# Steps to 1/std, the end of a convolution, and the halves of layer 3's convolutions: three edits in one kernel of four layers

## The chip, the cores and the metric

The kernel runs on one core of a Trainium2 chip. A core has five engines that run side by side, each through its own list of instructions in order: TensorE (PE in the profile; its weight loads are listed apart as PEld), VectorE (DVE), ScalarE (ACT), GpSimd (POOL) and SyncE (SP), which here only issues transfers. Transfers run on the core's 16 DMA engines. The engines meet through semaphores, and the profile shows for an idle engine what ended its wait.

The metric is the device time of one execution in microseconds, so lower is better. Three runs of the kernel before took 3970.76, 3970.90 and 3973.34 us; the median is 3970.9.

## The reference

`x` has the shape (1, 512, 64, 64) in fp32. Four layers follow one another, each a group norm, a function and a residual:

```python
def _gn(v, G=32, eps=1e-5):          # 32 groups of 16 channels, over all pixels
    m = jnp.mean(g, axis=(2, 3, 4), keepdims=True)
    s = jnp.var(g, axis=(2, 3, 4), keepdims=True)
    return ((g - m) / jnp.sqrt(s + eps)).reshape(v.shape)

x = x + L0(_gn(x)); x = x + L1(_gn(x)); x = x + L2(_gn(x)); x = x + L3(_gn(x))
```

- **L0** is attention with 8 heads of 64 over the 4096 pixels. Its scores are -(|q|^2 + |k|^2 - 2 q.k) / 8; q, k, v and the output are 1x1 convolutions of 512 to 512 channels.
- **L1 and L2** are gated convolutions. A 1x1 convolution takes 512 channels to 1024: the first 128 are `pwa`, the other 896 go through a 7x7 depthwise convolution and are cut into 128, 256 and 512 (`dw0`, `dw1`, `dw2`). Then `h = pwa * dw0`, `h = pw0(h) * dw1`, `h = pw1(h) * dw2`, and the layer's output is `w_out(h)`.
- **L3** is a linear attention. A 1x1 convolution takes 512 channels to 768, with a scale and a bias for each channel; a 5x5 depthwise convolution of these, with its own scales and biases, gives 768 more. Of the 1536, the first 512 are q, the next k, the last v; `q = relu(q) + eps`, `k = relu(k) + eps`. Then `vk` = sum over the pixels of v k^T, `attn = (vk q) / z` with `z` from the mean of k and q, `y = attn * g + bt + v`, and a 1x1 convolution `w_proj` of y with a scale and a bias.

The pointwise biases are inputs too, and there is no affine part in the group norms.

## The kernel before, in words

**What stays on chip.** `X` (128 partitions, 4 chunks of channels, 4096 pixels) holds the activations through all layers. A block is 512 pixels, of which there are eight.

**A layer's start.** `bn_stats` of every block were taken as the blocks of the layer before were finished. `_group_params` (L91) joins them (`bn_aggr`), has TensorE average them over each group of 16 channels with the constant matrix `gmask`, copies the mean out of PSUM (L100), forms the variance in three small VectorE operations (L105 to L107), sends it through `gmask` again, adds eps (L111), takes the square root on ScalarE (L113) and the reciprocal on VectorE (L115), and sharpens it in four small operations (L117 to L121). The product's input is not normalised: 1/std goes into the weights, one multiplication for each group of 128 output channels (L426 in layer 0, L819 in layers 1 and 2, L1021 in layer 3), the first on VectorE and the others on GpSimd. The mean is subtracted from `X` in place (`_Centered`, L319), block by block. `known` is called when the mean is there: it makes `less`, the negative mean (L335), centers the four chunks of the first block (two on ScalarE, two on GpSimd, L345 and L347), and adds the mean to `offset` (L338), from which the last layer gives it back. Later blocks are centered as they come up: on VectorE and ScalarE in layer 0, on ScalarE in layers 1 and 2, on VectorE in layer 3.

**Depthwise convolutions on TensorE** (`_PlaneConv`, L631). The image of a channel is cut into planes, with a border. A product over the input channels is evicted from PSUM into a `plane` tile (L843 on VectorE in layers 1 and 2; L1035 on ScalarE in layer 3) and written to DRAM from ScalarE's queue (`F` in layers 1 and 2, `G` in layer 3, L681). `load` (L686) fetches from there for two rounds of a convolution: the taps `T` (L690) and the pixels `S` (L707), both issued by SyncE. The 128 partitions of `S` are four groups of 32: two sets of channels, and for each set two shifts of the pixels. In layers 1 and 2 the second shift (in x) is a copy on ScalarE within `S` (L713); in layer 3 the second shift is in y, one tile row of taps lower, and is fetched from DRAM by a transfer of its own, so that a load there is one transfer of `T` and four of `S`. There are four buffers of each, and loads are issued one set ahead. `conv` (L721) runs the matmuls of 64 rows by 32 columns into two PSUM tiles, turns these into the right layout on VectorE (L767), and at its end goes over the result in four quarters: a transposition on VectorE (L773 in layers 1 and 2, L776 in layer 3) and a bias on ScalarE (L902, L1058). It is a generator: at each `yield` its caller puts other work between the convolution's matmuls.

**The order.** A tile scheduler orders the instructions of every engine, except the matmuls that go through `pc.matmul` (L657), which keep the order of the program. So which product stands between which parts of a convolution is written out by hand. In layers 1 and 2 `convolve` (L896) does it: there are seven convolutions, and the items of `between` (input products for the next convolutions, gates, output products) are dealt out evenly over `parts` slots, eight of them, one at each `yield`; seven lie between loads or turns and the last one behind the four quarters. After the seventh convolution the remaining gates and the output products of chunks 5 and 6 follow.

In layer 3 a convolution is one of six chunks `i` in one of two tile rows `hf`, written `(i, hf)`; it has two halves, one for each pair of PSUM tiles, each with two loads the loads of the first unit in a call of `convs` (L1065) are issued as it begins, those of each further unit while the one before it runs. `fill(n)` (L1047) makes the next n products of `w_qkv` with their planes; `made` has them chunk by chunk, in pairs for chunks 0 to 3. `gather(hf, q)` (L1081) takes a quarter of a tile row: it reads k's planes back (`row`), and gives four steps, each of which transposes k and v on TensorE (`ps_t`), evicts them (`kT` on ScalarE, `vT` on VectorE), makes a product with `w_proj` (`pv`, ScalarE, then added to `X` on GpSimd) and adds v k^T into four standing PSUM tiles (`vkp`). `added` (L1134) prepares the constant part of the output with 16 small products. The order of layer 3 is

```python
fill(20)
convs([(0, 0), (1, 0)], fills(3, 3, 3, 3))
fill(2)
convs([(2, 0), (3, 0), (4, 0)], fills(2, 2, 2, 2, 3, 3))
convs([(0, 1), (5, 0)], [added])
for q, units in enumerate(((1,), (2,), (3, 4), (5,))):
    convs([(i, 1) for i in units], gather(0, q))
```

so that all twelve convolutions have begun before the last quarter of tile row 0 is gathered, and the gathering of tile row 1 follows with no convolution beside it.

Of the kernel before, what the change touches and what calls it, by code (L numbers as in the profile page):

```python
# [16 lines left out]
P = 128  # L17
# [73 lines left out]
def _group_params(nc, small, psum, stats, gmask, known=None):  # L91


    mv = small.tile([P, NC, 2], FP, tag="gn_mv", name="gn_mv")
    for c in range(NC):
        nc.vector.bn_aggr(mv[:, c, :], stats[:, c, :, :].rearrange("p b s -> p (b s)"))
    ps = psum.tile([P, BLK], FP, tag="mm", name="gn_ps")
    nc.tensor.matmul(ps[:, 0:NC], gmask, mv[:, :, 0], start=True, stop=True)
    mean = small.tile([P, NC], FP, tag="gn_mean", name="gn_mean")
    nc.vector.tensor_copy(mean, ps[:, 0:NC])  # L100
    if known is not None:
        known(mean)

    d = small.tile([P, NC], FP, tag="gn_d", name="gn_d")
    nc.vector.tensor_sub(d, mv[:, :, 0], mean)  # L105
    nc.vector.tensor_mul(d, d, d)
    nc.vector.tensor_add(d, d, mv[:, :, 1])  # L107
    ps = psum.tile([P, BLK], FP, tag="mm", name="gn_ps")
    nc.tensor.matmul(ps[:, 0:NC], gmask, d, start=True, stop=True)
    a = small.tile([P, NC], FP, tag="gn_a", name="gn_a")  # L110
    nc.vector.tensor_scalar(a, ps[:, 0:NC], GN_EPS, None, ALU.add)  # L111
    s = small.tile([P, NC], FP, tag="gn_s", name="gn_s")
    nc.scalar.activation(s, a, AF.Sqrt)  # L113
    r = small.tile([P, NC], FP, tag="gn_r", name="gn_r")
    nc.vector.reciprocal(r, s)  # L115

    t = small.tile([P, NC], FP, tag="gn_t", name="gn_t")  # L117
    nc.vector.tensor_mul(t, r, r)
    nc.vector.tensor_mul(t, t, a)
    nc.vector.tensor_scalar(t, t, -0.5, 1.5, ALU.mult, ALU.add)  # L120
    nc.vector.tensor_mul(r, r, t)  # L121
    return mean, r


@with_exitstack
# [193 lines left out]
class _Centered:  # L319
# [10 lines left out]
    def first(self, view):  # L330


        def known(mean):
            self.less = self.small.tile([P, NC], FP, tag="less", name="less")
            self.nc.vector.tensor_scalar(self.less, mean, -1.0, None, ALU.mult)  # L335
            for c in range(NC):
                self.take(view(c), c, self.nc.gpsimd if c > 1 else self.nc.scalar)
            self.nc.vector.tensor_add(self.offset, self.offset, mean)  # L338

        return known  # L340

    def take(self, xs, c, eng):
        less = self.less[:, c : c + 1]
        if eng is self.nc.scalar:
            eng.activation(xs, xs, AF.Identity, bias=less)  # L345
        else:
            eng.tensor_scalar(xs, xs, less, None, ALU.add)  # L347


def _normalize(tc, X, gmask, small, psum, st):  # L350

    nc = tc.nc
    for b in range(NB):
        for c in range(NC):
            nc.vector.bn_stats(st[:, c, b, :], X[:, c, ts(b, BLK)])
    mean, rstd = _group_params(nc, small, psum, st, gmask)
    for b in range(NB):
        for c in range(NC):
            xs = X[:, c, ts(b, BLK)]
            nc.vector.tensor_scalar(  # L360
                xs, xs, mean[:, c : c + 1], rstd[:, c : c + 1], ALU.subtract, ALU.mult
            )


# [4 lines left out]
def _attention_pairs(tc, a, X, QO, gmask, small, centered, stats, okay):  # L369
# [19 lines left out]
    with tc.tile_pool(name="att1", bufs=1) as p1, tc.tile_pool(  # L389
# [32 lines left out]
        def project(pair):  # L422
            w = p1.tile([P, 3, NC, P], FP, tag="wqkv", name=f"wqkv{pair}")
            nc.sync.dma_start(out=w, in_=a["L0_wqkv"][pair])
            for n in range(3):
                eng = nc.vector if (pair, n) == (0, 0) else nc.gpsimd  # L426
                eng.tensor_tensor(
                    w[:, n], w[:, n], rstd.unsqueeze(2).to_broadcast([P, NC, P]), ALU.mult
                )
            Q = QO[pair]  # L430
            sq = []
            for b in range(NB):
                cols = ts(b, BLK)
                if pair == 0 and b:
                    for c in range(NC):
                        centered.take(X[:, c, cols], c, nc.scalar if c > 1 else nc.vector)
                if b % 2 == 0:
                    sq.append(ptp.tile([P, 2 * BLK], FP, tag="pt", name="sq"))
                for n in range(2):
                    ps = ps_s.tile([P, 2 * BLK], FP, tag="s", name="ps_qk")[:, 0:BLK]  # L440
                    for c in range(NC):
                        nc.tensor.matmul(  # L442
                            ps, w[:, n, c, :], X[:, c, cols], start=(c == 0), stop=(c == NC - 1)
                        )
                    if n == 0:
                        nc.scalar.activation(Q[:, cols], ps, AF.Copy, scale=2 * scale * gain_in)  # L446
                    else:
                        nc.vector.tensor_scalar(K[:, cols], ps, gain_in, None, ALU.mult)
                nc.scalar.activation(sq[-1][:, ts(b % 2, BLK)], Q[:, cols], AF.Square)
                ps = ps_s.tile([P, 2 * BLK], FP, tag="s", name="ps_v")[:, 0:BLK]  # L450
                for i in range(QT):
                    for c in range(NC):
                        nc.tensor.matmul(
                            ps[:, ts(i, P)],
                            X[:, c, ts(b * QT + i, P)],
                            w[:, 2, c, :],
                            start=(c == 0),
                            stop=(c == NC - 1),
                        )
                nc.vector.tensor_scalar(  # L460
                    V[:, ts(b, QT), :].rearrange("p t d -> p (t d)"), ps, gain_in, None, ALU.mult
                )
# [168 lines left out]
class _PlaneConv:  # L631
# [54 lines left out]
    def load(self, i, hf, wT, r):  # L686
# [4 lines left out]
            out=w.rearrange("p r g b m -> p r (g b m)"),  # L691
            in_=wT[i, r : r + nl].rearrange("r p x -> p r x"),
        )
        run = (f.part + f.by - 1) * f.fw
        S = self.sp3.tile([P, nl, 4, run], FP, tag="S", name="S")
        F = self.F[i]
        chan = f.planes * f.plane
        for rho in range(2):
            for jy in range(f.jy):
                src = bass.AP(  # L700
                    F.tensor,
                    F.offset
                    + (rho * f.nr + r) * 4 * f.ch * chan
                    + (hf * f.part + jy * f.by) * f.fw,
                    [[f.plane, 32], [f.ch * chan, 4 * nl], [1, run]],
                )
                nc.sync.dma_start(  # L707
                    out=S[ts(2 * rho + jy, 32)].rearrange("p r g n -> p (r g) n"), in_=src
                )
            if f.jx == 2:  # L710
                flat = S.rearrange("p r g n -> p (r g n)")
                n = 4 * nl * run - f.bx
                nc.scalar.copy(flat[ts(2 * rho + 1, 32), 0:n], flat[ts(2 * rho, 32), f.bx : f.bx + n])  # L713
        return w, S

    def ahead(self, i, hf, wT, r0=0):
# [4 lines left out]
    def conv(self, i, hf, wT, finish, dst, primed=False):  # L721
# [48 lines left out]
        for q in range(4):  # L770
# [7 lines left out]
                    self.turned[:, :, ts(q, f.phx), :].rearrange("p b l c -> p l b c"),  # L778
                )
            finish(d)  # L780
        yield


@with_exitstack
def _gated_convs(ctx, tc, a, X, vcol, gmask, small, new_stats, centered, stats, F):
# [12 lines left out]
    for layer in ("L1", "L2"):  # L798
# [16 lines left out]
        )  # L815
        stats = new_stats()

        def scaled(w, eng):
            eng.tensor_tensor(w, w, rstd.unsqueeze(2).to_broadcast([P, NC, P]), ALU.mult)  # L819
            return w  # L820

        scaled(w_in[0], nc.vector)
        for w in w_in[1:] + [w_gate]:
            scaled(w, nc.gpsimd)

        def product(w, hs):
            ps = ps_mm.tile([P, BLK], FP, tag="mm", name="ps")
# [8 lines left out]
        def fused(i, k):  # L836

            if i == 0 and k:
                for c in range(NC):
                    centered.take(pc.pixels(X[:, c, :], k), c, nc.scalar)  # L840
            pc.take(
                i, k, taking(w_in[i], k),
                lambda dst, src: nc.vector.tensor_scalar(  # L843
# [1 line left out]
                ),  # L845
            )
            if k == NB - 1 and len(w_in) < NDW:
                w_in.append(scaled(weights("w_in", 1 + len(w_in)), nc.gpsimd))

        D = {}  # L850

# [44 lines left out]
        def convolve(i, first, between):  # L896
# [8 lines left out]
            pc.ahead(i, 0, taps)  # L905
            for f in first:
                f()
            parts = FORM.nr // FORM.run
            done = 0
            for part, _ in enumerate(pc.conv(i, 0, taps, bias, D[i], True)):  # L910
                upto = len(between) * (part + 1) // parts
# [21 lines left out]
def _linear_attention(ctx, tc, a, X, vcol, vall, ident, gmask, small, centered, stats, F, Z, out):  # L933
# [49 lines left out]
    with ExitStack() as st:  # L983
# [33 lines left out]
                pc.matmul(ps, w(c), h, start=(c == 0), stop=(c == len(hs) - 1))  # L1017
            return ps

        def scaled(w, eng):  # L1020
            eng.tensor_tensor(w, w, rstd.unsqueeze(2).to_broadcast([P, NC, P]), ALU.mult)  # L1021

        for i, w in enumerate(w_qkv):
            scaled(w, nc.gpsimd if i else nc.vector)

        def fused(i, k):

            if i == 0 and k:
                for c in range(NC):
                    centered.take(pc.pixels(X[:, c, :], k), c, nc.vector)  # L1030
            w = w_qkv[i]
            ps = product(lambda c: w[:, c, :], [pc.pixels(X[:, c, :], k) for c in range(NC)])
            pc.take(
                i, k, ps,
                lambda dst, src: nc.scalar.activation(  # L1035
                    dst, src, AF.Identity,
                    bias=vcol(pre + "b_qkv", i), scale=vcol(pre + "s_qkv", i),
                ),
            )
            if k == NB - 1 and len(w_qkv) < NQKV:  # L1040
                w_qkv.append(weights(len(w_qkv)))
                scaled(w_qkv[-1], nc.gpsimd)

        made = [(i, k) for p in (0, 2) for k in range(NB) for i in (p, p + 1)]
        made += [(i, k) for i in (4, 5) for k in range(NB)]
# [105 lines left out]
        fill(20)  # L1151
        convs([(0, 0), (1, 0)], fills(3, 3, 3, 3))
        fill(2)
        convs([(2, 0), (3, 0), (4, 0)], fills(2, 2, 2, 2, 3, 3))
        convs([(0, 1), (5, 0)], [added])
        for q, units in enumerate(((1,), (2,), (3, 4), (5,))):
            convs([(i, 1) for i in units], gather(0, q))

        km = wp.tile([P, NC], FP, tag="km", name="km")
# [185 lines left out]
```

## Time and profile before

| | us |
|---|---|
| median of three runs | 3970.9 |
| the profiled execution | 3972.97 |
| its span (first to last instruction) | 3971.3 |
| TensorE busy | 3880.2 |
| VectorE busy | 2276.4 |
| ScalarE busy | 1871.9 |
| GpSimd busy | 95.6 |
| DMA: bytes moved | 232.84 MB |

The profiled execution had a mean granted TensorE clock of 0.989 of full speed. Its stages, by the first matmul of each layer: layer 0 begins at 36.05 us, layer 1 at 2306.33, layer 2 at 2817.53 and layer 3 at 3332.82; the last layer ends with the span.

How to read it: TensorE is busy for nearly the whole span, so the other engines' busy shares say little by themselves. What matters is where TensorE stands still or runs at less than full clock, and which instruction, on which engine, released it. The rows of stretches used below give for each engine the busy time with the number of instructions in brackets, and at the end the granted TensorE clock, the mean busy share of the DMA engines and GB/s. Rows of a timeline give the start, the duration, the engine, the line, the operation and its operands; in square brackets stands how long the engine had waited and for what.

### The profile page before, as it was taken

To read this page: it belongs to the slowest core of one execution; us is meant where nothing else is said; L and a number is where in the kernel's file an instruction comes from. 1 tells how busy PE (TensorE), PEld (TensorE's weight loads), DVE (VectorE), ACT (ScalarE), POOL (GpSimd) and SP (SyncE) were. 2 spreads that over 40 slices of the span, in tenths; PEclk is the share of its full clock that TensorE was granted. 3 is DMA by queue.
4 is the path that set the end of the run, shared out by engine and by line. 5 is a ranking of instruction groups with operands and counts; after the bars stand their busy time and mean duration, and the time that the engine had idled before them with its cause. 6 is when DMAs were issued, how large, how long until landed. Compare 5 with 4: busy or idle time off the path is not lost. (4 is left out here: it accounts for less than half of the span.)

```text
span 3971.3 us, 81238 instructions
## 1 busy us (share of the span) xinstructions
PE 3880.2 (98%) x35666; PEld 1732.5 (44%) x35666; DVE 2276.4 (57%) x2490; ACT 1871.9 (47%) x2678; POOL 95.6 (2%) x86
## 2 busy tenths in 40 slices
PE   6999999999999999999999989999999999989999
PEld 3533345333353333443333345554455544445544
DVE  4577763777727777547667623466434665233335
ACT  2577753777726777446656444441344521222210
POOL 0000000000000000000000010000000001001110
PEclk9999999999999999999999999999999999989999
DMA  2000000000000000000000045651256511696234
GB/s 96 9 2 1 1 1 9 1 1 1 1 1 9 1 2 1 1 9 1 1 1 1 1 145 163 179 144 46 85 154 179 157 45 51 178 213 142 72 92 143
DMA packets 240456, 232.84 MB, mean 59 GB/s; under 512 B 14921, under 2 KB 205641, under 8 KB 239969
## 3 DMA queue, kind: packets, MB, share of 16 engines
q1 hardware_dynamic: 213424, 168.82, 16.5%
q10 hardware_dynamic: 26640, 58.72, 4.1%
q8 instruction: 282, 4.62, 0.5%
q14 instruction: 78, 0.63, 0.1%
q0 software_dynamic: 32, 0.06, 0.0%
HBM read 167.76 MB, written 59.77 MB: 57 GB/s over the span
## 5 line engine op out<-in xcount | busy, mean ns | idle before, releaser
L495 ACT ACTIVATE pt<-ps_s,A 128x512 f32<-128x512 f32 x2048 | 1284.7, 686 | 556.4 <-PE ps_s L487 528.5
L566 DVE TENSOR_TENSOR acc<-acc,pt 128x1024 f32<-128x1024 f32 x960 | 1175.4, 1224 | 331.9 <-ACT pt L495 306.2
L505 PE MATMUL av<-pt,V 64*64 64x512 f32 x8192 | 1112.3, 590 | 0.9 <-ACT pt L495 0.9
L487 PE MATMUL ps_s<-O,K 64*64 64x512 f32 x8192 | 1111.4, 589 | 0.0
L505 PEld LDWEIGHTS av<-pt,V 64*64 64x64 f32 x8192 | 339.6, 133 | 557.4 <-issue 525.6
L487 PEld LDWEIGHTS ps_s<-O,K 64*64 64x64 f32 x8192 | 334.1, 133 | 554.1 <-issue 308.7
L713 ACT COPY S<-S 32x1295 f32<-32x1295 f32 x224 | 284.2, 1269 | 295.9 <-DMA S<-F 233.4
L657 PE MATMUL ps<-X,w_in_L 128*128 128x512 f32 x896 | 406.5, 606 | 6.8 <-DMA pw_L<-in_L_pw_dram 4.4
L657 PE MATMUL ps_cv<-S,T 64*32 64x128 f32 x13824 | 242.7, 277 | 15.4 <-DMA S<-G 14.7
L657 PEld LDWEIGHTS ps<-X,w_in_L 128*128 128x128 f32 x896 | 167.1, 192 | 206.8 <-issue 196.3
L843 DVE TENSOR_SCALAR plane<-ps,vec 128x512 f32<-128x512 f32 x112 | 83.4, 748 | 301.2 <-PE ps L657 230.4
L657 PEld LDWEIGHTS ps_cv<-S,T 64*32 64x32 f32 x13824 | 199.5, 107 | 122.9 <-issue 75.2
L442 PE MATMUL ps_qk<-X,wqkv 128*128 128x512 f32 x512 | 228.1, 599 | 5.6 <-issue 5.6
L657 PE MATMUL ps<-h,w_out_L 128*128 128x512 f32 x512 | 227.9, 598 | 0.0
L657 PE MATMUL ps<-X,w_qkv 128*128 128x512 f32 x384 | 170.7, 603 | 5.2 <-DVE w_qkv L1021 5.2
L767 DVE STREAM_TRANSPOSE turned<-ps_cv 128x512 f32<-128x512 f32 x48 | 31.6, 697 | 226.6 <-PE ps_cv L657 226.6
L345 ACT ACTIVATE X<-X,less 128x512 f32<-128x512 f32 x78 | 49.5, 708 | 230.1 <-DVE less L335 218.5
L657 PE MATMUL ps<-h,pw_L 128*128 128x512 f32 x320 | 149.3, 619 | 7.4 <-DVE X L881 6.2
L446 ACT ACTIVATE O<-ps_qk 128x512 f32<-128x512 f32 x32 | 19.1, 597 | 272.5 <-PE ps_qk L442 272.5
L442 PEld LDWEIGHTS ps_qk<-X,wqkv 128*128 128x128 f32 x512 | 95.9, 192 | 116.9 <-issue 116.9
L657 PEld LDWEIGHTS ps<-h,w_out_L 128*128 128x128 f32 x512 | 95.0, 190 | 114.6 <-issue 106.5
L865 DVE SCALAR_TENSOR_TENSOR h<-ps,vec,h 128x512 f32<-128x512 f32 x112 | 82.4, 745 | 104.7 <-PE ps L657 101.4
(129 smaller groups left out, 2540.3 us busy)
## 6 DMA issues: line engine op xcount, KB each, us to landing
T<-in_L_T_dram SPq DMA_DIRECT2D x112, 384.0 KB, 3.9
F<-plane ACTq DMA_DIRECT2D x112, 324.0 KB, 2.9
S<-F SPq DMA_DIRECT2D x224, 162.0 KB, 4.3
S<-G SPq DMA_DIRECT2D x192, 136.0 KB, 4.3
row<-G SPq DMA_DIRECT2D x80, 272.0 KB, 4.0
G<-plane ACTq DMA_DIRECT2D x48, 289.0 KB, 2.9
T<-in_L_T_dram SPq DMA_DIRECT2D x48, 256.0 KB, 4.3
out_dram<-y SPq DMA_DIRECT2D x32, 256.0 KB, 2.1
```

Source lines behind the costliest of these rows:

```text
L345: eng.activation(xs, xs, AF.Identity, bias=less)
L442: nc.tensor.matmul(ps, w[:, n, c, :], X[:, c, cols], start=(c == 0), stop=(c == NC - 1))
L446: nc.scalar.activation(Q[:, cols], ps, AF.Copy, scale=2 * scale * gain_in)
L487: nc.tensor.matmul(ps[ts(half, D), ts(h, BLK)], K[rows, t * P + half * D : t * P + (half + 1) * D], QO[pair][rows, cols], start=True, stop ...
L495: nc.scalar.activation(pt[:, ts(h, BLK)], ps[:, ts(h, BLK)], AF.Exp, bias=A[:, t, h : h + 1])
L505: nc.tensor.matmul(av[half][rows, :], V[keys, t, rows], pt[keys, ts(h, BLK)], start=(t == 0), stop=(t == NT - 1),)
L566: nc.vector.tensor_add(acc, acc, pt)
L657: self.tc.keep_in_program_order(self.nc.tensor.matmul(*args, **kw))
L713: nc.scalar.copy(flat[ts(2 * rho + 1, 32), 0:n], flat[ts(2 * rho, 32), f.bx : f.bx + n])
L767: nc.vector.transpose(out, src)
L843: lambda dst, src: nc.vector.tensor_scalar(dst, src, vcol(pre + "b_in", 1 + i), None, ALU.add),
L865: nc.vector.scalar_tensor_tensor(d, ps, bias, d, ALU.add, ALU.mult)
```

## The change

**Steps to 1/std.** `less` is read from PSUM at once, in place of the copy of the mean; the variance adds it in place of subtracting the mean. `known` is called after the second product with `gmask`. The first block's chunks are centered by ScalarE (two), GpSimd and VectorE (one each), all later blocks by ScalarE in every layer, layer 3 included. `offset` is kept up by `began`, called after the first weight is scaled. The other weights are scaled on ScalarE, in four activations of 128 columns with a scale for each partition, where before one operation on GpSimd did it (in layer 0 the later pairs of heads stay on GpSimd). Layer 3's planes are evicted on VectorE in place of ScalarE.

**Layer 3's second tile row of taps.** A load fetches each set's pixels once, 153 KB in place of two transfers of 136 KB, and ScalarE copies them, shifted by a row of taps, to the other 32 partitions. The convolutions of tile row 0 are all done in one call, and those of tile row 1 are spread over the four quarters of the gathering.

**A convolution's end.** In layers 1 and 2 there is a `yield` after each of the four quarters, and the items between are dealt out over 11 slots in place of eight.

```diff
-    mean = small.tile([P, NC], FP, tag="gn_mean", name="gn_mean")
-    nc.vector.tensor_copy(mean, ps[:, 0:NC])
-    if known is not None:
-        known(mean)
+    less = small.tile([P, NC], FP, tag="gn_less", name="gn_less")
+    nc.vector.tensor_scalar(less, ps[:, 0:NC], -1.0, None, ALU.mult)
...
-    nc.vector.tensor_sub(d, mv[:, :, 0], mean)
+    nc.vector.tensor_add(d, mv[:, :, 0], less)
...
     nc.tensor.matmul(ps[:, 0:NC], gmask, d, start=True, stop=True)
+    if known is not None:
+        known(less)
...
-            self.less = self.small.tile([P, NC], FP, tag="less", name="less")
-            self.nc.vector.tensor_scalar(self.less, mean, -1.0, None, ALU.mult)
+            self.less = less
             for c in range(NC):
-                self.take(view(c), c, self.nc.gpsimd if c > 1 else self.nc.scalar)
-            self.nc.vector.tensor_add(self.offset, self.offset, mean)
+                self.take(view(c), c, (None, None, self.nc.gpsimd, self.nc.vector)[c])
...
+    def began(self):
+        self.nc.vector.tensor_sub(self.offset, self.offset, self.less)
...
+    def scaled(self, w, rstd, eng):
+        if eng is self.nc.scalar:
+            for c in range(NC):
+                eng.activation(w[:, c], w[:, c], AF.Copy, scale=rstd[:, c : c + 1])
+        else:
+            shape = [P, NC, w.shape[-1]]
+            eng.tensor_tensor(w, w, rstd.unsqueeze(2).to_broadcast(shape), ALU.mult)
+        return w
...
-                eng = nc.vector if (pair, n) == (0, 0) else nc.gpsimd
-                eng.tensor_tensor(
-                    w[:, n], w[:, n], rstd.unsqueeze(2).to_broadcast([P, NC, P]), ALU.mult
+                centered.scaled(
+                    w[:, n], rstd, nc.gpsimd if pair else nc.scalar if n else nc.vector
                 )
+            if pair == 0:
+                centered.began()
...
-        run = (f.part + f.by - 1) * f.fw
+        run = (f.part + f.by - 1 + (f.jy - 1) * f.by) * f.fw
...
+        step = f.bx if f.jx == 2 else f.by * f.fw
+        n = 4 * nl * run - step
         for rho in range(2):
-            for jy in range(f.jy):
...
+            nc.sync.dma_start(
+                out=S[ts(2 * rho, 32)].rearrange("p r g n -> p (r g) n"), in_=src
+            )
+            nc.scalar.copy(flat[ts(2 * rho + 1, 32), 0:n], flat[ts(2 * rho, 32), step : step + n])
...
             finish(d)
-        yield
+            if f.parts == 1 or q == 3:
+                yield
...
-            scaled(w, nc.gpsimd)
+            centered.scaled(w, rstd, nc.scalar)
...
-            parts = FORM.nr // FORM.run
+            parts = FORM.nr // FORM.run + 3
...
-            scaled(w, nc.gpsimd if i else nc.vector)
+            centered.scaled(w, rstd, nc.scalar if i else nc.vector)
+        centered.began()
...
-                    centered.take(pc.pixels(X[:, c, :], k), c, nc.vector)
+                    centered.take(pc.pixels(X[:, c, :], k), c)
...
-                lambda dst, src: nc.scalar.activation(
-                    dst, src, AF.Identity,
-                    bias=vcol(pre + "b_qkv", i), scale=vcol(pre + "s_qkv", i),
+                lambda dst, src: nc.vector.tensor_scalar(
+                    dst, src, vcol(pre + "s_qkv", i), vcol(pre + "b_qkv", i), ALU.mult, ALU.add
                 ),
...
-        convs([(2, 0), (3, 0), (4, 0)], fills(2, 2, 2, 2, 3, 3))
-        convs([(0, 1), (5, 0)], [added])
-        for q, units in enumerate(((1,), (2,), (3, 4), (5,))):
+        convs([(2, 0), (3, 0), (4, 0), (5, 0)], fills(2, 2, 2, 2, 6) + [added])
+        for q, units in enumerate(((0,), (1, 2), (3,), (4, 5))):
             convs([(i, 1) for i in units], gather(0, q))
```

## The prediction

> **What bounds the kernel now.** I read the page first, then a table of stretches, then the timeline inside the bad stretches. The page's busy time:
>
> ```profile
> PE 3880.2 (98%) x35666; PEld 1732.5 (44%) x35666; DVE 2276.4 (57%) x2490; ACT 1871.9 (47%) x2678; POOL 95.6 (2%) x86
> ```
>
> TensorE sets the end, so an edit is worth only the PE idle time, or half-speed PE time, that it takes away. Idle is 3971.3 - 3880.2 = 91 us. The stretches (length, then busy us of PE, PEld, DVE, ACT, POOL, then PEclk, DMA share, GB/s) show where:
>
> ```profile
> 0.00:41.55 41.55, 6.65 (x11) 3.44 (x12) 32.38 (x70) 12.68 (x19) 9.06 (x14) 1.00 0.64 229
> 2292.81:2311.41 18.60, 6.20 (x11) 3.19 (x11) 5.99 (x20) 10.89 (x18) 9.82 (x9) 0.63 0.61 208
> 2717.78:2724.42 6.64, 4.55 (x15) 1.81 (x10) 6.59 (x7) 2.96 (x3) 0.00 (x0) 1.00 0.37 98
> 2724.42:2731.25 6.83, 5.82 (x7) 2.52 (x8) 3.50 (x6) 1.57 (x2) 0.00 (x0) 0.50 0.01 3
> 3322.77:3338.82 16.05, 6.95 (x12) 3.32 (x12) 15.66 (x43) 1.54 (x3) 10.08 (x9) 0.57 0.36 132
> 3530.61:3566.20 35.59, 24.12 (x548) 18.14 (x544) 17.80 (x30) 6.51 (x8) 0.00 (x0) 0.54 1.12 216
> ```
>
> Three kinds of place: the steps to 1/std before a layer, the end of a layer's last convolution (2717, 3232), and layer 3's convolutions at 3530, where DMA runs at a share over 1. In the last three rows PEclk near 0.5 is half speed. Timeline, VectorE, steps to 1/std of layer 3:
>
> ```profile
> 3326.90 0.89 DVE L347 TENSOR_SCALAR X<-X,less 128x512 f32<-128x512 f32 x1
> 3327.71 0.14 DVE L111 TENSOR_SCALAR gn_a<-gn_ps 128x4 f32<-128x4 f32 x1
> 3327.77 1.97 DVE L347 TENSOR_SCALAR X<-X,less 128x512 f32<-128x512 f32 x3
> 3329.67 0.16 DVE L115 RECIPROCAL gn_r<-gn_s 128x4 f32<-128x4 f32 x1
> ```
>
> The Sqrt ended at 3328.09, yet the reciprocal starts 1.6 us later, behind three centerings of X. Timeline at the end of layer 1's last convolution:
>
> ```profile
> 2720.22 4.59 DVE L773 STREAM_TRANSPOSE h<-h 128x1024 f32<-128x1024 f32 x4
> 2725.43 1.22 PE L657 MATMUL ps<-h,pw_L 128*128 128x512 f32 x1 [3.10 <-DVE X L881]
> ```
>
> Four transpositions in a row hold the evictions; PE runs out of its four PSUM buffers for 3.10 us. SyncE's queue in layer 3:
>
> ```profile
> 3545.05 0.39 SPq L690 DMA_DIRECT2D T<-in_L_T_dram  x1
> 3545.66 2.75 SPq L707 DMA_DIRECT2D S<-G  x4
> ```
>
> One load of taps and pixels per 4 us (eight from 3535 to 3567), where half a convolution, which takes two loads, computes for 2.05 us.
>
> **What the skill says.** "TensorE: Matmul & The Clock Gate" (What's actually happening): the clock halves after an idle window of 3.4 us, the windows run free. The trace agrees: half-speed stretches of 6.83, 10.24, 13.65 and 34.13 us. So a gap costs itself plus about 3 us. "GPSIMD Engine Reference" (Specifications): its SBUF interface is shared with VectorE. Agrees: the same weight scaling takes VectorE 0.69 us at 2816.69, 1.50 at 2304.72 while GpSimd scales. "DMA: Bandwidth & Descriptors" (Specifications) puts line rate at 512 B and more; here 544 B packets of S took 28 ns at 3405-3440, 49 ns at 3535-3580.
>
> **Part 1, steps to 1/std.** In the built order, VectorE keeps one centering (X, chunk 3) ahead of the square; the rest goes to ScalarE, as do the other weights' scalings, four ACTIVATEs of 128 columns each. From Sqrt to first matmul undisturbed is 2817.53 - 2815.38 = 2.15 us (layer 2).
> - Layer 0: Sqrt is bound by ScalarE: 28.25 + two centerings 1.33 + table load 1.28 = 30.9. First matmul 33.05 against 36.05: -3.0.
> - Layer 3: 25.37 add; one centering holds 0.4 to 0.8; matmul near 26.4; +0.68 and +0.17 as before: Sqrt 27.25, matmul 29.4 against 32.82: -3.4 (-3.2 to -3.6).
> - Layer 1: Sqrt 0.25 earlier (still behind the table load); scaling 0.69 for 1.50: -1.05.
> - Layer 2: saved 0.2 against the centering's 0.4: 0 (+-0.2).
> Sum -7.5. The added ACTIVATEs: "ScalarE: Activation LUTs" (What ACT_TABLE_LOAD costs) gives 186 + 93 + 0.833 N ns, 93 overlapped: an estimate of 0.29 us each, 16 of them 4.7 us; no row shows this size, the 128x512 centering is 0.708. Costed at nothing: a block of four products lasts 3.44 us on PE (6.9 at half speed), ScalarE's work for it is 4 x 0.617 + 0.33 = 2.8. The tightest is the next block's last centering: layer 1 ready 2310.5, wanted 2311.7; layer 2, behind the issue of a plane, 2826.0 against 2826.6. Uncovered it costs up to 2 us each. Evictions of q, k, v planes move from ScalarE (0.78) to VectorE (0.75), which is free then.
>
> **Part 2, convolution ends.** Yields after each quarter put output products between the transpositions; VectorE's order follows. Layer's last convolution: 15 products (0.86 us each) stand after its last rows, VectorE: turns 1.94, then 4 x 1.13 and 15 x 0.6 in groups 1,3,3,4,4. Product n waits for eviction n-4: the sum of PE waits is 0.7, none over 0.5. So 3.1 becomes 0.7, and half speed (5.8 us busy, 2.9 lost) goes: -5.3. The end of the sixth convolution, 12 products: 1.4 for 0.61; of the fourth, eight products of 0.86: 0.9 for 0. Net -3.6 per layer, -7.2 for two. What is thinned out elsewhere: between loads of layers 1 and 2 PE has 4.1 us and more on average, the load needs 2.5 us of ScalarE's copies and 3.3 of DMA (708 KB at 212 GB/s), and four buffers are full at a start: nothing.
>
> **Part 3, layer 3.** A load was four S transfers of 136 KB; now two of 153 KB and two ScalarE copies of 1207 elements, 1.19 us each (1.269 for 1295). DMA time by packets: before (1024 x 49 + 256 x 73)/16 = 4.3 us, after (512 x 51 + 256 x 73)/16 = 2.8; SyncE issues 1.4 for 2.35; ScalarE 2.4. So 4.0 us per load becomes 2.8. But convolution 5's planes are now complete only t (its last product) and its loads queue on SyncE behind three `row` transfers that wait for the same planes: planes land t+4.1, rows 4.7, taps and first S 2.8, plus 1: t+12.6; copies: first load usable t+14.2, then one per 2.4, fourth t+21.4. The second load of (0,1) is copied after convolution 5's four affines in ScalarE's order, which wait for VectorE's turns and transpositions (7 us after its end): its end t+32. Without waits it would be t+12.65: 19.3 lost. Before, 35.59 us held 4.43 + 4 x 2.05: 23.0 lost. Earlier, (2,0) to (4,0): before the halves took 0.9, 0.9, 2.5 and 1.3 too long, 5.6. After, the starts of (2,0) and (4,0) need fresh planes, then transfer, then copies: 2.1 and 4.5, the others nothing: 6.6. Net -2.6. After that, each half has a step of 7.74 us beside it and ScalarE 7.3 of 9.8 us: kT and pv stand behind copies, kT has 3.4 us of slack under the `w_proj` products: nothing; uncovered, up to 2 us per step.
>
> **Sum.** -7.5 - 7.2 - 2.6 = -17.3 against the profiled execution: span 3971.3 (time 3973.0, 1.7 around it) to 3954. That execution is 2.1 over the median of the runs, 3970.9; I take the difference from the median: 3953.6, so **3954**.
>
> **Rivals.**
> - B, the transfers really go under: saturated packets at 49 ns fall back to 28, copies keep up, 14 of the 19.3 vanish. For: 33% fewer bytes where DMA share is 1.12. Against: fresh planes and rows come first. 3940.
> - C, layer 3 turns against it: copy waits for transfer, transfer waits for buffer, both in order; 4 us per load again and longer starts, 8 us over before: -7.5 - 7.2 + 8: 3964.
> - E, the conv ends give nothing: the evictions are spread into many short waits, half speed stays: -17.3 + 7.2: 3961.
> - D, slower: in the 16 steps of the gather, ScalarE waits on a copy while kT stands behind it, PE then waits for kT. Each step would have to lose 1.6 us to pass +8 in all; at 2 us, 32 - 14.7 = +17: 3988. Against it: copies have two halves (19.6 us) of lead.
>
> **How the numbers follow.** Chances: forecast 0.52 (own range 3948 to 3960), B 0.17, C 0.13, E 0.10, D 0.08. Range 3938 to 3966 leaves out D and part of B and C. 0.2% (8 us) is about what a measurement tells from no change: faster 0.80 (forecast, B, E and little of C), same 0.12, slower 0.08.
>
> **What would show it.** First matmul near 33.0; starts of layers 1 to 3 at -1, 0, -3.4 relative to their last product; no PE gap over 1 us at the layers' last convolutions and no half-speed stretch of 6.83 there; S transfers of 153 KB, 96 of them, and 96 copies of 1.19 us; PE waiting in layer 3 on ScalarE's S instead of DMA S, some 20 us in one place after the last w_qkv product. It is wrong if PE waits in the gather on kT, or if ScalarE's scalings hold the first blocks.

## The result and the profile after

The changed kernel took 3967.47 us (median of 14 runs, 3965.76 to 3970.76), the kernel before, run beside it, 3969.83 (14 runs, 3963.32 to 3973.34). The ratio is 0.9996 with a 95% interval of 0.9988 to 1.0003: no difference that can be measured. The forecast was 3954.

The profiled execution of the changed kernel took 3965.76 us, its span is 3964.0, which is 7.3 us less than that of before. But the profile of before came from a run 3 us over its median and that of after from one 1.7 us under its own, so most of these 7.3 us are a difference between two executions. First the page's busy times of the changed kernel:

```profile
PE 3871.1 (98%) x35666; PEld 1727.7 (44%) x35666; DVE 2290.3 (58%) x2496; ACT 2001.5 (50%) x2852; POOL 65.7 (2%) x61
```

TensorE's idle time is 3964.0 - 3871.1 = 92.9 us; it was 91. What was taken away in some places has come back in others. The same table of stretches as before (length, busy us of PE, PEld, DVE, ACT, POOL, then PEclk, DMA share, GB/s), for the changed kernel:

```profile
0.00:38.15 38.15, 6.68 (x11) 3.48 (x12) 25.05 (x56) 11.47 (x22) 4.09 (x11) 1.00 0.69 249
2289.31:2304.60 15.29, 4.06 (x9) 2.41 (x9) 5.49 (x20) 7.85 (x19) 3.06 (x3) 0.67 0.54 172
2568.07:2590.00 21.93, 19.21 (x522) 11.41 (x529) 9.21 (x12) 13.08 (x11) 0.00 (x0) 1.00 0.70 191
2710.33:2723.98 13.65, 13.51 (x35) 5.39 (x31) 13.59 (x19) 4.06 (x4) 0.00 (x0) 1.00 0.10 30
3316.84:3328.60 11.76, 5.60 (x11) 2.78 (x11) 5.10 (x22) 7.93 (x20) 3.99 (x5) 0.71 0.52 180
3520.71:3551.71 31.00, 18.30 (x421) 14.26 (x417) 13.97 (x24) 21.94 (x21) 0.00 (x0) 0.59 0.67 168
```

The first, second and fifth rows are the starts of layers 0, 1 and 3, shorter than before. The fourth is the end of layer 1's last convolution: 13.51 us of 13.65 busy at full clock, where before PE stood still for 3.1 us and then ran at half speed. The third is new: in the middle of layer 1, where PE never waited before, it is idle for 2.7 us of 22. In the last row, ahead of layer 3's gathering, the DMA share has fallen to 0.67 from 1.12, and ScalarE is busy for 22 us of 31. The place (called the hole below) is 31.0 us long for 35.6, but it holds three halves of convolutions for four.

A layer's start is from the last product of the layer before to the first product of this one, its body from there to its last product, both worked out from the matmuls' times in the trace:

| stretch | before, us | after, us | measured | forecast |
|---|---|---|---|---|
| start of layer 0 | 36.05 | 32.61 | -3.4 | -3.0 |
| start of layer 1 | 13.52 | 12.35 | -1.2 | -1.05 |
| body of layer 1 | 504.64 | 504.96 | +0.3 | -3.6 |
| start of layer 2 | 6.56 | 6.70 | +0.1 | 0 |
| body of layer 2 | 505.24 | 503.52 | -1.7 | -3.6 |
| start of layer 3 | 10.04 | 6.91 | -3.1 | -3.4 |
| body of layer 3 | 638.44 | 640.28 | +1.8 | -2.6 |

The starts are right to 0.2 us in their sum (-7.6 for -7.5). The bodies failed: +0.4 for -9.8. Each column is one profile, and a single profile gives layer 3's body only to about 3 us: it took 640.7 and 637.9 us in two kernels of the experiments below (e1_start, e8_deal_old_l3) that have the same program there. Two timelines of the changed kernel on VectorE show what did work, first the steps to 1/std of layer 3:

```profile
3319.52 0.48 DVE L348 TENSOR_SCALAR X<-X,gn_less 128x512 f32<-128x512 f32 x1
...
3321.11 0.16 DVE L111 TENSOR_SCALAR gn_a<-gn_ps 128x4 f32<-128x4 f32 x1 [0.48 <-PE gn_ps L107]
3321.55 0.18 DVE L115 RECIPROCAL gn_r<-gn_s 128x4 f32<-128x4 f32 x1 [0.27 <-ACT gn_s L113]
```

One centering of 0.48 us is left among the small steps, and the reciprocal follows the square root after 0.27 us. Then the end of layer 1's last convolution:

```profile
2712.17 0.67 DVE L888 TENSOR_TENSOR X<-X,ps 128x512 f32<-128x512 f32 x1
2712.76 1.22 DVE L782 STREAM_TRANSPOSE h<-h 128x1024 f32<-128x1024 f32 x1
2713.90 1.84 DVE L888 TENSOR_TENSOR X<-X,ps 128x512 f32<-128x512 f32 x3
2715.67 1.23 DVE L782 STREAM_TRANSPOSE h<-h 128x1024 f32<-128x1024 f32 x1
2716.82 1.85 DVE L888 TENSOR_TENSOR X<-X,ps 128x512 f32<-128x512 f32 x3
2718.59 1.23 DVE L782 STREAM_TRANSPOSE h<-h 128x1024 f32<-128x1024 f32 x1
2719.74 2.44 DVE L888 TENSOR_TENSOR X<-X,ps 128x512 f32<-128x512 f32 x4
2722.11 1.23 DVE L782 STREAM_TRANSPOSE h<-h 128x1024 f32<-128x1024 f32 x1
2723.26 2.44 DVE L888 TENSOR_TENSOR X<-X,ps 128x512 f32<-128x512 f32 x4
```

Evictions now stand between the transpositions, in the groups of 1, 3, 3, 4 and 4 that the forecast worked with.

### The profile page after: what moved, and what is told of

It is laid out like the page before. It is cut to its first block, busy times and chain, and to the rows that moved or that the text cites. A ratio compares the mean times of both kernels' runs of the same rounds, so it can differ in the third digit from the quotient of the medians.

```text
span 3964.0 us, 81294 instructions
## 1 busy us (share of the span) xinstructions
PE 3871.1 (98%) x35666; PEld 1727.7 (44%) x35666; DVE 2290.3 (58%) x2496; ACT 2001.5 (50%) x2852; POOL 65.7 (2%) x61
## 5 line engine op out<-in xcount | busy, mean ns | idle before, releaser
L722 ACT COPY S<-S 32x1295 f32<-32x1295 f32 (+1 forms) x320 | 399.0, 1247 | 316.5 <-DMA S<-F 197.4
L346 ACT ACTIVATE X<-X,gn_less 128x512 f32<-128x512 f32 x120 | 76.9, 709 | 226.4 <-DVE gn_less L100 211.0
L776 DVE STREAM_TRANSPOSE h<-ps_cv 128x512 f32<-128x512 f32 x112 | 109.1, 1046 | 48.7 <-PE ps_cv L669 48.7
```

The lines of the kernel that those rows point to most:

```text
L346: self.nc.scalar.activation(xs, xs, AF.Identity, bias=less)
L776: nc.vector.transpose(out, src)
```

## The experiments

All times are medians; the ratio is to the kernel before, run beside it. Parts 1, 2 and 3 are those of the prediction: the steps to 1/std, the ends of convolutions, layer 3.

| kernel | what it is | us | ratio, 95% interval |
|---|---|---|---|
| e1_start | part 1 alone | 3959.84 | 0.9980, 0.9974 to 0.9987 |
| e2_ends | part 2 alone | 3969.44 | 1.0001, 0.9995 to 1.0008 |
| e3_layer3 | part 3 alone | 3974.94 | 1.0014, 1.0008 to 1.0021 |
| e4_deal | after, items dealt otherwise | 3954.51 | 0.9964, 0.9951 to 0.9978 |
| e8_deal_old_l3 | e4, layer 3: old loads, old order | 3952.85 | 0.9956, 0.9943 to 0.9970 |
| e7_deal_old_order | e4, layer 3: new loads, old order | 3952.72 | 0.9958, 0.9945 to 0.9972 |
| e9_deal_old_loads | e4, layer 3: old loads, new order | 3946.25 | 0.9942, 0.9928 to 0.9955 |
| e10_split | e4, layer 3's copies on two engines | 3946.60 | 0.9945, 0.9931 to 0.9958 |
| e11_01_first | e9, (0,1) ahead of (5,0) | 3952.95 | 0.9958, 0.9945 to 0.9972 |
| e13_ahead | e10, (0,1)'s first loads earlier | 3949.54 | 0.9950, 0.9937 to 0.9964 |
| e14_split12 | after, layers 1 and 2's copies on two engines | 3964.72 | 0.9991, 0.9984 to 0.9997 |

The kernel before had medians of 3968.07 to 3970.92 beside these, so times of kernels that were not run side by side can differ by 2 to 3 us without a cause in the kernel.

### Each part alone

e1_start is the changed kernel with the diff's second and third part taken back, that is, the old `load`, the old order of layer 3, one `yield` behind the four quarters and eight slots.

> Only the steps to 1/std (with the scalings, centerings and layer 3's plane eviction that go with them). If the prediction's part 1 holds by itself, as the starts of the changed kernel's layers say (-3.4, -1.2, +0.1, -3.1 us), the time is 7.5 us under before: 3962. Rival: the starts of before differ from run to run with the half-speed windows, and the profiled run showed a bad one: then only 3 to 5 us, 3965 to 3967. In both, the bodies of layers 1 to 3 keep their length within 1 us.

Measured: 3959.84, 8.2 us under before. The starts of its profile differ from before's by -3.4, -1.5, -0.1 and -3.1 us, as in the changed kernel. So part 1 is worth about what the forecast said. One thing was expected by no theory: the bodies of layers 1 and 2 are 500.9 and 501.5 us long and not 504.6 and 505.2, with their gaps of 3.1 us at the last convolution's end unchanged. It is taken up below.

e2_ends and e3_layer3 are the kernel before with one part of the diff added:

```diff
-        yield
+            if f.parts == 1 or q == 3:
+                yield
...
-            parts = FORM.nr // FORM.run
+            parts = FORM.nr // FORM.run + 3
```

> Only the yields at a convolution's end with the items dealt over 11 slots. Theory of thinning: the end's gap and half-speed stretch go (about -7 us a layer where both are seen), but the same waits of PE for S appear as in the changed kernel (5.7 us in layer 1, 3.3 in layer 2), so -1.4 us in all: 3968. The prediction: -7.2 us, 3963, and no wait for S in layers 1 and 2. Rival: the waits for S in the changed kernel come from the scalings and centerings that part 1 put on ScalarE; then they are absent here too and the time is 3963 or less.

Measured: 3969.44, no difference. The waits of PE inside the convolutions are there too (5.1 us in layer 1, 2.1 in layer 2), though ScalarE has no scalings here. That rules out the rival and fits the thinning. One of these waits, of 1.64 us, was followed by half speed for 3.41 us, so such a wait can cost more than itself.

> Only layer 3's copy on chip and its new order of convolutions; planes are still evicted on ScalarE. By the changed kernel's profile layer 3's body is 1.8 us longer: +1.8, up to +5 as ScalarE has planes and copies: 3972 to 3975. The prediction's -2.6 would be 3967. In the trace: about 20 us lost ahead of the first gathering step, waits of 3 us in the gathering for kT and vT.

Measured: 3974.94, 6.9 us over before; the body of layer 3 is 644.6 us for 638.4. Part 3 alone makes the kernel slower. The three parts alone add up to -8.2 + 1.4 + 6.9 = +0.1, the change measured -2.4.

### The slots that were thinned out

With 11 slots in place of eight, each slot between two loads gets fewer items. Of ten items, the integer division gives the first slot none; of eight, it leaves three slots empty. There two loads' matmuls follow one another with nothing between. The timeline of PE and ScalarE in the changed kernel at such a place, in layer 1's fifth convolution:

```profile
2580.77 0.59 PE L669 MATMUL ps<-X,w_in_L 128*128 128x512 f32 x1
2581.29 2.91 PE L669 MATMUL ps_cv<-S,T 64*32 64x128 f32 x181
2585.76 0.44 PE L669 MATMUL ps_cv<-S,T 64*32 64x128 f32 x11 [1.56 <-issue]
...
2582.18 0.33 ACTq L693 DMA_DIRECT2D F<-plane  x1
2582.66 2.56 ACT L722 COPY S<-S 32x1295 f32<-32x1295 f32 x2 [1.65 <-DMA S<-F]
```

192 matmuls are two loads. ScalarE waited 1.65 us, by the profile for the second load's pixels, its two copies end at 2585.22, and PE goes on at 2585.76. e4_deal deals the items of convolutions 0 to 4 as before up to the seventh slot, and spreads only the last eighth over the four quarters:

```diff
-                upto = len(between) * (part + 1) // parts
+                if i < 5 and part >= 7:
+                    early = len(between) * 7 // 8
+                    upto = early + (len(between) - early) * (part - 6) // 4
+                elif i < 5:
+                    upto = len(between) * (part + 1) // 8
+                else:
+                    upto = len(between) * (part + 1) // parts
```

> The changed kernel, but for convolutions 0 to 4 of layers 1 and 2 the first seven slots get an eighth of the items each, as before, and only the last eighth is spread over the four quarters; convolutions 5 and 6 keep 11 equal slots. Theory of thinning: the waits for S inside convolutions (5.7 us in layer 1, 3.3 in layer 2) go and the ends stay good: 8 to 9 us under the changed kernel, 3959. Rival (the copies are late because of ScalarE's added work): the waits stay, 3967.

Measured: 3954.51, 13.0 us under the changed kernel. The same place in its profile (timeline of PE):

```profile
2579.78 1.59 PE L669 MATMUL ps_cv<-S,T 64*32 64x128 f32 x96
2581.30 3.70 PE L669 MATMUL ps<-X,w_in_L 128*128 128x512 f32 x8
2584.93 1.59 PE L669 MATMUL ps_cv<-S,T 64*32 64x128 f32 x96
```

A product stands between any two loads, and PE doesn't wait for S anywhere in layers 1 and 2. Their bodies are 499.7 and 499.5 us, 5.2 and 4.0 shorter than in the changed kernel, and the ends kept their 0.85 us of short waits. So the dealing was the cause of the waits. The remaining 3.8 us of the 13.0 lie outside these two layers or between executions.

e14_split12 asks which resource gives out in the thinned slots. In layers 1 and 2 the second set's copy goes to VectorE:

```diff
-            nc.scalar.copy(flat[ts(2 * rho + 1, 32), 0:n], flat[ts(2 * rho, 32), step : step + n])
+            src, dst = flat[ts(2 * rho, 32), step : step + n], flat[ts(2 * rho + 1, 32), 0:n]
+            if f.jx == 1 or rho == 0:
+                nc.scalar.copy(dst, src)
+            else:
+                nc.vector.tensor_copy(dst, src)
```

> The changed kernel, but in layers 1 and 2 one of the two copies of a load runs on VectorE and one on ScalarE, so that a load's copying takes half as long. If ScalarE's copying (2.5 us a load, behind the issues of planes) is what makes PE wait for S in the thinned-out slots, the waits of 5.7 and 3.3 us fall under 3 in all and the time is 6 us lower, 3961. If it is the transfers (708 KB a load, at 207 us of KB per ns some 3.4 us where a slot is 3.4 us long, and four buffers), the waits stay at 6 us or more, 3965 to 3968.

(207 KB per us is meant there.) Measured: 3964.72, 2.7 us under the changed kernel, with intervals of the two ratios that overlap. In the profiles, one of each and this one of its fastest run, the waits are 4.3 + 1.2 = 5.5 us for 5.7 + 3.3 = 9.1. So copying seems to be a part of it, over a third, and the rest stays with half the copying: at the place shown above PE even waits 1.9 us for 1.6. Whether the rest is the transfers' rate or the four buffers is open; a fifth buffer was not tried.

### Layer 3: which half of part 3 costs

Part 3 has two halves, the loads with copies and the order. e8 takes back both from e4_deal, e7 the order alone, e9 the loads alone.

> The kernel e4_deal with layer 3's loads and order as before (two transfers for each set, no copies; (0,1) ahead of (5,0)). If part 3 costs here what it costs alone (+6.9 us), 3954.5 - 6.9 = 3948. If its cost in e3_layer3 came from ScalarE evicting planes as well, which e4_deal no longer does, the time stays at 3953 to 3955.

> e4_deal with the old order of layer 3's convolutions, but the new loads (copies on chip). Theory of order: the loss sits in the 20 us ahead of the gathering, where (0,1) waits for planes just written, then rows, transfers and copies; with (0,1) ahead of (5,0) its loads are there in time and the smaller loads come every 2.8 us for 4.0: 6 to 9 us under e8_deal_old_l3, about 3941. Theory of copies: ScalarE's copies (2.4 us a load, in order behind affines) hold the convolutions and the gathering in either order: 3950 to 3955.

> e4_deal with the new order of layer 3's convolutions, but the old loads (transfers only). Theory of order: the hole ahead of the gathering stays and gets longer, as six loads at 4.0 us take 7 us more than at 2.8: 3958 to 3962. Theory of copies: without them the hole shrinks and the gathering has no waits: 3946 to 3950.

| | old order | new order |
|---|---|---|
| transfers only | 3952.85 (e8) | 3946.25 (e9) |
| copies on ScalarE | 3952.72 (e7) | 3954.51 (e4) |

My theory of the order was wrong: the new order gains 6.6 us with the old loads (e9 against e8), and the new loads lose 8.3 with it and nothing without it. In the old order they lose 2.3 us ahead of `added` and gain 1.8 in the hole (e7 and e8, one profile each). e8 also asked whether part 3 costs beside part 1 what it costs alone, 6.9 us. It doesn't: e4 is 1.7 us over e8, less than their intervals can tell from nothing. Part 1 takes the evictions of the planes off ScalarE; that this makes the difference was not tested by itself. The waits of PE in layer 3 (engine, tile and line, what it waited for, us in total, times, longest), first in e4_deal:

```profile
PE ps_cv L669 <- ACT S L722: 17.3, 13, 3.9
...
PE vkp L669 <- DVE vT L1112: 1.9, 2, 1.3
...
PE vkp L669 <- ACT kT L1110: 0.7, 1, 0.7
```

and in e9_deal_old_loads:

```profile
PE ps_cv L669 <- DMA S<-G: 11.5, 12, 2.2
...
PE vkp L669 <- DVE vT L1115: 0.6, 1, 0.6
```

In place of transfers PE waits for copies, and longer. By place, from the two profiles: the first half of (4,0) takes 5.2 us too long with copies and 0.9 with transfers (4.3); the products behind it 23.1 us for 20.9, as half speed followed the wait (2.2); the hole, here and below counted from the end of `added`, 25.6 for 23.7 (1.9); the gathering waits 2.6 for 0.6 (2.0); other halves give 2.1 back. That is 8.3, as much as the medians differ by; the bodies of layer 3 in the two profiles differ by 10.0, so 1.7 of these are not placed. Why the order gains: with it three halves of convolutions, six loads, stand in the hole, and in e8 four with eight loads. The hole of e9 in the table of stretches, `added` included,

```profile
3505.40:3532.79 27.39, 17.93 (x421) 13.66 (x417) 14.03 (x24) 6.51 (x8) 0.00 (x0) 0.59 1.09 213
```

has a DMA share of 1.09 at 213 GB/s, and PE waits there for transfers. So I read each load fewer there as a gain; the next kernel has more of them.

e11_01_first puts a further unit into the hole of e9:

```diff
-        convs([(2, 0), (3, 0), (4, 0), (5, 0)], fills(2, 2, 2, 2, 6) + [added])
-        for q, units in enumerate(((0,), (1, 2), (3,), (4, 5))):
+        convs([(2, 0), (3, 0), (4, 0), (0, 1), (5, 0)], fills(2, 2, 2, 2, 6) + [added])
+        for q, units in enumerate(((1,), (2,), (3, 4), (5,))):
```

> e9_deal_old_loads, but (0,1) stands between (4,0) and (5,0) in the same call, so that it and not (5,0) is what comes when chunk 5's planes have just been written. If the DMA rate sets the hole (six loads of 4.0 us there), (0,1)'s first half comes out of it for nothing and the time is 2 to 4 us under e9_deal_old_loads: 3942 to 3944. If the order of e9 is as good because fewer halves stand ahead of the gathering, a further half there costs its 2 loads, up to 8 us: 3950 to 3954, as e8_deal_old_l3.

Measured: 3952.95, the second alternative: five halves now run in one go ahead of the gathering and take 36.3 us. With transfers only, the hole thus takes 23.7 us for three halves (e9), 30.4 for four (e8) and 36.3 for five, some 6 to 7 us for each half with its two loads, at 213 to 216 GB/s in all three.

e10_split leaves e4_deal's order and loads, and takes half of layer 3's copies to VectorE (`f.jx == 2` for `f.jx == 1` in the diff of e14_split12).

> e4_deal (new loads, new order), but of the two copies of a load in layer 3 one runs on VectorE, one on ScalarE. Theory of copies: ScalarE, busy 8.8 of 9.0 us in the middle of the hole ahead of the gathering, sets the pace of the loads there; with half of the copies away the hole of about 26 us gets 5 to 8 us shorter and ScalarE has room: 3947 to 3950. Rival: it is the chain of each load (transfer of some 4 us, then a copy, each behind the one before) and the fresh planes; then the split gives 2 us at most: 3953 to 3955.

Measured: 3946.60, 7.9 us under e4_deal: with half the copying on ScalarE the loss is gone. The time is that of my theory, the place is not. The hole stayed at 25.1 us. The gain is at (4,0)'s first half (2.4 us too long with what stands ahead of it, for 5.2), the products behind it (20.9 us, no half speed) and the gathering. On VectorE such a copy takes 0.78 us in the median (0.88 in the mean), on ScalarE 1.20.

In e10_split one wait of 7.3 us remains in the hole, for copies that stand in order behind (5,0)'s transpositions and affines. e13_ahead issues them earlier:

```diff
-        def convs(units, between):
+        def convs(units, between, primed=False):
...
-                for part, _ in enumerate(conv(*u, n > 0)):
+                for part, _ in enumerate(conv(*u, n > 0 or primed)):
...
-        convs([(2, 0), (3, 0), (4, 0), (5, 0)], fills(2, 2, 2, 2, 6) + [added])
+        convs([(2, 0), (3, 0), (4, 0), (5, 0)], fills(2, 2, 2, 2, 6) + [added, lambda: pc.ahead(0, 1, a["L3_T"])])
...
-            convs([(i, 1) for i in units], gather(0, q))
+            convs([(i, 1) for i in units], gather(0, q), q == 0)
```

> e10_split, with the loads and copies of (0,1)'s first half issued in the program while (5,0)'s first half runs, as it is for every unit inside one call, and not behind (5,0)'s end. In e10_split PE waits 7.3 us for them in the hole: both copies stand in order behind (5,0)'s turns, transpositions and affines. Theory of order on VectorE and ScalarE: that wait falls to 1 to 2 us, the body of layer 3 is 5 to 6 us shorter, 3941. Rival: the transfer is as late as the copies (four buffers, each freed only as PE goes on); then 2 us at most, 3945.

Measured: 3949.54, not under e10_split. The wait of 7.3 us became three of 3.0, 2.1 and 1.0, and the hole is 25.05 us for 25.08. Earlier issue doesn't help, as the rival said. What the hole consists of beyond the fresh planes, the buffers and the rate of loads wasn't separated further.

### A gap and the clock's windows

e1_start's bodies of layers 1 and 2 were 3.7 us shorter than before's with the same gaps. So the kernel before was profiled once more.

> The kernel before once more, for a second profile. The half-speed stretches behind the gap of 3.1 us at the last convolution's end in layers 1 and 2 were in its first profile and not in that of e1_start, which has the same gap. If they depend on where the gap falls against the clock's windows, this profile may have them or not, and a body of layer 1 or 2 without them is 3.5 to 4 us shorter (501 for 504.6 us); the gap itself stays at 3.1 us. If they come with the gap in this kernel, both are there again.

Measured: 3967.05 us in its one run, the body of layer 1 is 501.4 us, that of layer 2 504.6. The table of stretches of this second profile, over the gaps of layer 1 (first two rows) and layer 2:

```profile
2715.82:2722.12 6.30, 4.56 (x14) 1.81 (x10) 6.25 (x7) 2.62 (x3) 0.00 (x0) 1.00 0.35 89
2722.12:2728.95 6.83, 5.48 (x13) 2.58 (x14) 4.59 (x7) 1.90 (x2) 0.00 (x0) 1.00 0.04 16
3223.88:3230.70 6.82, 4.76 (x30) 1.82 (x11) 6.56 (x7) 2.94 (x3) 0.00 (x0) 1.00 0.50 156
3230.70:3237.53 6.83, 5.79 (x7) 2.50 (x8) 3.52 (x6) 1.59 (x2) 0.00 (x0) 0.50 0.00 0
```

The gap is 3.09 us in both layers, yet PEclk behind it is 1.00 in layer 1 and 0.50 in layer 2. All half-speed stretches of a profile begin on one grid of 3.41 us, and from profile to profile the grid has no fixed place against the kernel. Laid over the eight gaps of this kind in four profiles (before, twice; e1_start; e3_layer3), the larger share of the gap that falls into one window of the grid is 1.74, 1.79 and 1.93 us where full speed stayed, and 2.06, 2.09, 2.15, 2.16 and 2.47 us where half speed followed. This is no sharp limit for other places: where small matmuls that the profile counts as busy stood in the same window, half speed also followed 1.92 us (before, start of layer 2) and 1.91 (the same place in e3_layer3), and in e2_ends the 1.64 us above.

## Why the prediction was wrong

**Part 1, steps to 1/std: right.** First matmul at 32.61 us (33.05 forecast); starts of -3.4, -1.2, +0.1 and -3.1 us; alone 8.2 us. The added ACTIVATEs, an estimate of 0.29 us each from the Trainium skill, "ScalarE: Activation LUTs" (What ACT_TABLE_LOAD costs), took 2.43 us for eight in layer 0, 0.30 each: the trace agrees. They held no first block.

**Part 2, the ends: right at the ends themselves, wrong in two terms.** In layer 1 the waits at the seventh convolution's end are 0.13 us (0.7 forecast), at the sixth's 0.72 (1.4) and at the fourth's none (0.9), 0.85 in all, and no half-speed stretch is left there; the ends came out better than forecast. The step that failed is "What is thinned out elsewhere ... nothing". I compared the average of 4.1 us between loads with what a load needs. But the items are dealt by integer division, so some slots get none, and in others only two gates stand between two loads, which then come 3.4 us apart. PE waited 5.7 us for S in layer 1 and 3.3 in layer 2, where it had not waited before. The second term is half speed behind the gap of 3.1 us, which I took as certain at 2.9 us a layer because the one profile showed it in both. From the Trainium skill, "TensorE: Matmul & The Clock Gate" (What's actually happening), I had that the windows run free, and did not draw the consequence: half speed depends on where the gap falls, and behind these eight gaps it followed in five. That section has the clock drop after an idle window of about 3.4 us; here 2.06 us of one window were enough, so the measurement decides.

In the profiled pair, layer 1's account is: idle +3.1, half speed -4.0, and a remainder of +1.2 in time that the profile counts as busy, which was not split further; sum +0.3. Layer 2's is +1.4 - 4.4 + 1.2, about -1.7.

That also fits a median that moved by 2.4 us only, when part 1 gives 8.2. By one profile each, part 1 alone leaves layers 1 and 2 at 500.9 and 501.5 us, and the changed kernel has 505.0 and 503.5: +6.1. Part 3 adds 1.7 (e4 against e8). With these, -8.2 + 6.1 + 1.7 is -0.4, against -2.4 with an interval of -4.8 to +1.2.

**Part 3, layer 3: the sizes at the hole right, the gain not there.** The starts of (2,0) and (4,0) lost 1.6 and 4.7 us (2.1 and 4.5 forecast), the hole 20.4 (19.3), together 26.7 for 25.9. What failed is "After that ... nothing": the gathering waited 2.9 us, in three steps, for `vT` behind the transpositions of a convolution's end on VectorE and for `kT` behind copies on ScalarE. The timeline of ScalarE in one of them:

```profile
3648.28 0.76 ACT L1112 ACTIVATE pv<-ps,pbias,vec 128x512 f32<-128x512 f32 x1
3649.07 2.42 ACT L722 COPY S<-S 32x1207 f32<-32x1207 f32 x2
3651.51 0.69 ACT L1104 ACTIVATE kT<-ps_t,eps 128x512 f32<-128x512 f32 x1
```

`kT` waits for two copies, and `vkp` on PE for `kT` (1.0 us). The wait for `kT` is the mechanism of rival D: it is 1.0 us, and all three waits are a ninth of the 16 times 1.6 us that D needed. Part 3 was forecast at -2.6; alone it measured +6.9 (e3), and beside part 1 it gains nothing (+1.7, e4 against e8). And the reasons were turned round: I booked the smaller loads as the gain and the order as the loss. By the four kernels the order gains 6.6 us, and the copies take 8.3 back.

**The rivals.** B's saturated packets did fall back (the DMA share in the hole is 0.67), but PE then waited for ScalarE. C's time (3964) was near by luck: it put a loss of 8 us into layer 3 alone, where the profiled pair shows 1.8, and the hole didn't grow. E was right that the ends would give nothing on balance, wrong about why. Most of the 17.3 us was within reach: e4_deal, with the items dealt otherwise, is 13.6 us under before, run beside it.

**A version that beats both.** e9_deal_old_loads (part 1, the four yields with the other dealing, the new order, the old loads) takes 3946.25 us, 0.9942 of before.

## What to carry to other kernels

When work is spread over more slots, list what each slot gets: an average hides the empty ones, and a slot between two loads that gets nothing is a wait where there was none. A copy on chip in place of a transfer moves the load from the DMA engines to an engine with an order; count its time on that engine at the tightest place, and ask what stands behind it. And a half-speed stretch behind a gap shorter than the clock's grid (3.41 us here), seen in one profile, may be chance: look at a second profile before it is booked as a cost.

## What the runs showed of the hardware

A gap of 3.1 us on TensorE brought half speed for 6.83 us (two windows of 3.41) only where at least 2.06 us of it fell into one window, and not where the larger share was 1.93 us or less (eight gaps, four profiles; other places differ, as said above). The body of a layer was 3 to 4 us longer with it. It doesn't by itself explain the scatter between executions: 10.2 us in 21 runs of e1_start, which has the gap, but 9.1 and 8.8 in as many of e2_ends and e14_split12, which have not. A copy of 32 partitions by 1207 elements took 1.20 us on ScalarE and, in the median, 0.78 on VectorE, so the engine that the change chose for the copies was the slower one for them.
